# Layer 0 of a four-layer network: products with B and C taken for two tiles at once, through one PSUM tile of two halves

## The chip, the cores and the metric

The kernel runs on one core of a Trainium2 chip. The metric is the device time of one execution in microseconds (us). The core has five engines that work side by side, each through its own instructions in order: TensorE (PE, matrix products into PSUM), VectorE (DVE), ScalarE (ACT), GpSimd (POOL) and SyncE (SP), whose queue here issues the DMA transfers. PSUM is the small memory that TensorE writes; VectorE and ScalarE read and write it too. SBUF is the large on-chip memory. An engine that needs another's result waits on a semaphore for it, and everything behind it in its own queue waits too.

## What is computed

The input is x of shape (4, 96, 64, 64). Four layers follow each other. The change touches only the first, a block of two Mamba layers over sequences of L = 4096 positions, with 192 channels and 16 states per channel. Cut to what matters:

```
for i in range(2):
    h  = layernorm(seq) * ln_g + ln_b
    xs, z = split(h @ in_w)
    xc = silu(causal_conv4(xs) + conv_b)
    dt, Bm, Cm = split(xc @ xproj_w)            # 6, 16, 16 columns
    delta = softplus(dt @ dt_w + dt_b)
    dA  = exp(delta[..., None] * A)             # 192 channels x 16 states
    dBx = delta[..., None] * Bm[:, :, None, :] * xc[..., None]
    hstates = scan(h_t = dA_t * h_{t-1} + dBx_t)
    y   = einsum(hstates, Cm) + Dp * xc
    seq = seq + (y * silu(z)) @ out_w
out = batchnorm(fus_w @ concat(seq, gp(x)) + fus_b) + x
```

The three layers after it (a convolution with an MLP, an attention with a quantized MLP, a Fourier mixer with a quantized MLP) are the same in both kernels.

## The kernel before, in words

Everything is in 32-bit floating point in layer 0. The sequence is cut into pieces of T = 1024 positions. The work is a list of 32 items, one for each batch entry b (4), piece s (4) and Mamba layer i (2). Within an item the 192 channels x 16 states are 24 tiles of 128 partitions by 1024 columns: p (0 to 2) picks 64 channels, j (0, 1) one half of these, g (0 to 3) four of the states, so that a tile holds 32 channels x 4 states. The eight tiles of a p are taken in the order of the list `eight`, here (g, j) = (0,0), (0,1), (3,0), (1,1), (1,0), (3,1), (2,0), (2,1).

For each tile, `exp` (L464) makes dA on ACT from a replicated delta (ddb). The product delta * xc * B is made in one of two ways. On 16 tiles of an item, `rep` (L450) spreads four rows of B over the partitions with two matrix products of 512 columns each (four matmul records) into PSUM, and `scan` (L482) multiplies with the replicated delta * xc (udb) on VectorE, into PSUM. On the eight tiles in `pool_tiles` (2, 5, 7, 10, 13, 15, 18, 21), GpSimd makes the product in SBUF (`times_b`, L470, from udb and brep), and dA goes to PSUM instead (dap). Then `scan` runs the recurrence on VectorE (L486) into hs. `times_c` (L492) multiplies hs with C on GpSimd, in place, `sum_y` (L511) adds over states on PE, `gate` (L522) multiplies with silu(z) on VectorE, and `project` (L529, L224) and `finish` bring the item back to the sequence.

In PSUM there are two tiles of 1024 columns with one buffer each: tag "x" for rep, tag "u" for dap and for those products that are not written over rep. A group of tiles that share B starts at the tiles in `group_starts` (0, 3, 6, 8, 11, 14, 16, 19, 22): there `rep` is filled anew, nine times in an item.

`first_stage` prepares an item ahead: layer norm (L276 to L321), convolution (`parts_of` "xc"), xproj, delta, z, the transfers of delta and delta * xc to memory (dd, ud) and back, spread over the partitions (`load_d`), and of B and C (`load_b`, `load_c`). Its steps have slots; slot t of an item stands 24 steps before step t of that item. Weights and constants are set up before that by `prepare`.

The order on PE, VectorE, ACT and GpSimd is the program's own, written out by hand: the last loop of `layer0` goes over m, one step for each tile, and at each step calls scan(m), rep or exp for tile m+1, exp for tile m+3, times_c for tile m-1, the state copy (`keep_state`) for m-3, times_b by `b_slots`, then sum_y, gate, project and finish of the item at hand, and the steps of `first_stage` that are due. SP's order follows from the order of the calls. Waits are put in by the framework from what each instruction reads and writes in which tile.

Of the kernel before, what the change touches and what calls it, by code (L numbers as in the profile page):

```python
# [50 lines left out]
class Net:  # L51
# [43 lines left out]
    def layer0(self, dram, scratch):  # L95
        tc, nc, ins = self.tc, self.nc, self.ins
        x_in = ins["x"]
        with ExitStack() as ctx:
            cp = ctx.enter_context(tc.tile_pool(name="l0c", bufs=1))
            psum = ctx.enter_context(tc.tile_pool(name="l0p", bufs=2, space=PSUM))  # L100
            psum_x = ctx.enter_context(tc.tile_pool(name="l0x", bufs=1, space=PSUM))
            psum_y = ctx.enter_context(tc.tile_pool(name="l0y", bufs=2, space=PSUM))
# [11 lines left out]
            def wide(rows, cols, k):  # L114
                return psum_x.tile([128, T], F32, name="w_ps", tag="xu"[k % 2])[:rows, :cols]
# [113 lines left out]
            def global_pool():  # L229

                for b in range(B):
                    for s in range(NSC):
                        xt = wk.tile([128, T + 1], F32, name="gp_x", tag="hs", bufs=9)[:C, :T]
                        nc.sync.dma_start(xt, x_in[b, :, s * T : (s + 1) * T])
                        k = b * NSC + s
                        nc.vector.reduce_sum(pooled[:, k : k + 1], xt, axis=mybir.AxisListType.X)
                    yield
                pool4 = cp.tile([C, B], F32, name="pool4")
                nc.vector.reduce_sum(pool4, pooled.rearrange("p (b s) -> p b s", b=B), axis=mybir.AxisListType.X)
                ps = small(C, B)  # L240
                nc.tensor.matmul(ps, gpw, pool4, start=True, stop=True)
                gp = cp.tile([C, B], F32, name="gp")
                nc.scalar.activation(gp, ps, AF.Relu, scale=1.0 / L, bias=self.v("gp_b"))
                yield
                ps = small(C, B)
                nc.tensor.matmul(ps, fus[:, 1, :], gp, start=True, stop=True)
                nc.scalar.activation(fbias, ps, AF.Identity, bias=self.v("fus_b"))
                yield
# [6 lines left out]
            def first_stage(k):  # L255
# [11 lines left out]
                @at_slot(-11)  # L267
                def _():
                    m["xn"] = load_x(b, s, i) if k else x0


                @at_slot(-6)
                def _():
                    m["ps"] = [tile_ps(128), tile_ps(128)]
                    for q in range(8):
                        nc.tensor.matmul(  # L276
                            m["ps"][q // 4][:, q % 4 * C : q % 4 * C + C],
                            m["xn"][:, q * 128 : q * 128 + 128],
                            self.center,
                            start=True,  # L280
                            stop=True,
                        )

                @at_slot(-5)
                def _():
                    m["nt"] = cp.tile([128, 8, C], F32, name="nt", tag="nt")
# [11 lines left out]
                @at_slot(-4)  # L298
                def _():
                    for q in range(8):  # L300
                        x = m["ps"][q // 4][:, q % 4 * C : q % 4 * C + C]
                        nc.scalar.mul(m["nt"][:, q], x, m["rs"][:, q : q + 1])

                @at_slot(-3)
# [7 lines left out]
                @at_slot(-2)  # L312
# [23 lines left out]
                parts_of("xc", [(w_x[:, i, k], k) for k in range(4)], n, ((-1, 1), (0, 2), (2, 4)), 2)  # L336

                @at_slot(4)
                def _():
                    nc.scalar.activation(m["xc"], m["xc"], AF.Silu)  # L340
                    exp_set()

# [3 lines left out]
                @at_slot(7)  # L346
# [4 lines left out]
                @at_slot(8)  # L351
# [6 lines left out]
                parts_of("delta", [(dtw[:, i], 0)], dbl, ((9, 10), (9, 10), (10, 11)), 1)  # L358

                @at_slot(11)  # L360
# [4 lines left out]
                parts_of("z", [(w_z[:, i], 3)], n, ((11, 12), (12, 13), (13, 14)), 3)  # L365

                @at_slot(12)
                def _():
                    m["dd"] = dram.tile([DIN, T], F32, name="dd", tag="dd", bufs=2)
                    for at, rows in both:  # L370
                        nc.sync.dma_start(m["dd"].rearrange("(p c) t -> c p t", p=3)[:, :, at], m["delta"][rows])

                def du(p):
                    if p == 0:
                        m["ud"] = dram.tile([DIN, T], F32, name="ud", tag="ud", bufs=2)
                    of = slice(p, p + 1)
                    u = wk.tile([128, 1, MB], F32, name="du", tag="du")
                    nc.gpsimd.tensor_mul(u, m["delta"][:, of], m["xc"][:, of])  # L378
                    to = m["ud"].rearrange("(p c) t -> c p t", p=3)[:, of]
                    for at, rows in both:  # L380
                        nc.sync.dma_start(to[:, :, at], u[rows])

                for p in range(3):
                    at_slot(14 + 3 * p)(lambda p=p: du(p))

                @at_slot(16)
                def _():
                    nc.scalar.activation(m["z"], m["z"], AF.Silu)
                    exp_set()


                for p in range(3):
                    for j in range(2):
                        at_slot((16, 24, 32)[p] + j)(lambda p=p, j=j: load_d(m, "dd", p, j))
                        at_slot((18, 26, 34)[p] + j)(lambda p=p, j=j: load_d(m, "ud", p, j))
                for g, t in ((0, 10), (1, 21), (3, 23), (2, 25)):
                    at_slot(t)(lambda g=g: load_c(m, g))
                at_slot(19)(lambda: load_b(m, 3))
                at_slot(15)(lambda: load_b(m, 2))
                return steps  # L400

# [9 lines left out]
            def load_c(made, g):  # L411
                made["crep", g] = load_s(made, "crep", NST + 4 * g, 5)
# [4 lines left out]
            def load_d(made, k, p, j):  # L417

                t = wk.tile([128, T], F32, name=f"{k}b", tag=f"{k}b", bufs=4)
                row = 64 * p + 32 * j  # L420
                for s4 in range(4):
                    nc.sync.dma_start(t[32 * s4 : 32 * s4 + 32], made[k][row : row + 32])
                made[k, p, j] = t
# [5 lines left out]
            eight = [(0, 0), (0, 1), (3, 0), (1, 1), (1, 0), (3, 1), (2, 0), (2, 1)]  # L429
            order = [(p, g, j) for p in range(3) for g, j in eight]  # L430
            pool_tiles = (2, 5, 7, 10, 13, 15, 18, 21)
            group_starts = (0, 3, 6, 8, 11, 14, 16, 19, 22)
            NTL = len(order)
# [9 lines left out]
            def rep(m):  # L443

                k, t = divmod(m, NTL)
                x = psum_x.tile([128, T], F32, name="rep", tag="x")
# [6 lines left out]
                return x  # L453

            def exp(m):
# [3 lines left out]
                if on_pool(m):  # L459
                    da = psum_x.tile([128, T], F32, name="dap", tag="u")  # L460
# [5 lines left out]
            def times_b(m):  # L466
                k, t = divmod(m, NTL)
                h, g, j = order[t]
                u = made[k]["u", t] = wk.tile([128, T], F32, name="up", tag="up", bufs=2)
                nc.gpsimd.tensor_mul(u, made[k]["ud", h, j], made[k]["brep", g])  # L470

            def scan(m, x):
# [4 lines left out]
                if on_pool(m):  # L477
                    u = made[k].pop(("u", t))
                else:

                    u = x if on_pool(m + 1) else psum_x.tile([128, T], F32, name="u", tag="u")
                    nc.vector.tensor_mul(u, made[k]["ud", h, j], x)  # L482
                hs = made[k]["hs", t] = wk.tile([128, T + 1], F32, name="hs", tag="hs", bufs=9)
# [4 lines left out]
            def times_c(m):  # L488

                k, t = divmod(m, NTL)  # L490
                hs = made[k]["hs", t]
                nc.gpsimd.tensor_mul(hs[:, :T], hs[:, 1:], made[k]["crep", order[t][1]])  # L492

            def keep_state(m):
                k, t = divmod(m, NTL)
                b, s, i = items[k]
                col = column(t)
                if s < NSC - 1:
                    nc.scalar.copy(state[:, b, i, col : col + 1], made[k]["hs", t][:, T:])
# [5 lines left out]
            def sum_y(k, t0):  # L505

                for q, at in enumerate(halves):
                    for t in (t0, t0 + 1):
                        p, g, j = order[t]
# [4 lines left out]
                            made[k]["hs", t][:, at],  # L514
# [40 lines left out]
            b_slots = {2: 5, 4: 7, 7: 10, 9: 13, 12: 15, 15: 18, 18: 21, 23: NTL + 2}  # L555
# [3 lines left out]
            for m in sorted(stages[0])[:4]:  # L559
                for f in stages[0].pop(m):  # L560
                    f()
            prepare()
            wk = ctx.enter_context(tc.tile_pool(name="l0w", bufs=1))
            with tc.manual_schedule(engines=engines):
                gp = global_pool()
                first = min(stages[0])
                for m in range(first, last + 19):
                    k, t = divmod(m, NTL)
                    if 0 <= m < last:
                        scan(m, x)  # L570
                    if 0 <= m + 1 < last:
                        if on_pool(m + 1):
                            exp(m + 1)
                        elif (t + 1) % NTL in group_starts:
                            x = rep(m + 1)
                    if 0 <= m + AHEAD < last and not on_pool(m + AHEAD):
                        exp(m + AHEAD)
                    if 1 <= m <= last:
                        times_c(m - 1)
                    if 3 <= m < last + 3:  # L580
                        keep_state(m - 3)
                    if -1 <= m and t in b_slots and m - t + b_slots[t] < last:
                        times_b(m - t + b_slots[t])
                    for k0 in range(max(k - 1, 0), min(k + 1, len(items))):
                        at = m - NTL * k0
                        for p in range(3):
# [3 lines left out]
                            if at - 8 * p in (4, 6, 8, 10):  # L590
                                sum_y(k0, at - 4)
                            if at == 8 * p + 11:
                                gate(k0, p)
                        if at == 34:
                            made[k0]["x"] = load_x(*items[k0])
                        if at == 39:
                            project(k0)
                        if at == 41:
# [4 lines left out]
                    if m in (-20, -17, -14, -11, 15, 16):  # L603
# [878 lines left out]
```

## Time and profile before

| | us |
|---|---|
| median of three runs | 3914.21 (3908.41 to 3924.87) |
| profiled execution | 3925.66 |
| its span, first to last instruction | 3923.9 |
| PE busy in the span | 3205.9 (82%) |
| VectorE busy | 3154.4 (80%) |
| ACT busy | 2420.6 (62%) |
| GpSimd busy | 2911.4 (74%) |
| first scan of layer 0 starts | 77.3 |
| last scan of layer 0 ends | 2612.5 |

The page of the profile gives the busy time of each engine over the whole span, so it mixes layer 0 with the three others. Layer 0 takes the first two thirds. What the change does to it is read from stretches inside layer 0 and from groups of instructions that occur only there. A group's line reads: line of the kernel, engine, operation, the tile written <- the tiles read, shapes, count | busy us, mean ns of one | idle time of the engine just before them, and who ended it. "<-DVE hs L486 428.3" behind a group thus means that its engine stood idle for 428.3 us in total until a scan at L486 let it go. Idle time of an engine costs something only if another one then waits for it.

### The profile page before, as it was taken

The numbers are of one execution on the slowest core, as the hardware profiler recorded it, in microseconds if no ns is written. First come the engines' busy times: TensorE is split into PE (matmuls) and PEld (weight loads), VectorE is DVE, ScalarE is ACT, GpSimd is POOL, SyncE is SP. The second block draws the span as 40 slices with busy tenths as digits, with TensorE's granted clock in tenths as the row PEclk, the third lists the DMA queues.
The fourth block names the chain that finished last, engine by engine and source line by source line (L and its number), as shares of the span: only waits on it lengthen the run. The fifth ranks groups of instructions, "written<-read, shape, count | busy, mean of one in ns | idle before, by whom it ended". The sixth has DMA issues, their size and how long they took to land. (4 is left out here: it accounts for less than half of the span.)

```text
span 3923.9 us, 43975 instructions
## 1 busy us (share of the span) xinstructions
PE 3205.9 (82%) x13534; PEld 1294.8 (33%) x13534; DVE 3154.4 (80%) x2772; ACT 2420.6 (62%) x4644; POOL 2911.4 (74%) x1443
## 2 busy tenths in 40 slices
PE   6887878877878788877878887755899988899988
PEld 3222222222222222222222222115644534666643
DVE  5999999999999999999999999973374385444649
ACT  4666667766766676666766666532254676666557
POOL 2999999999999999999999999961101064444427
PEclk7788878898788888888878878766899999999989
DMA  7567656675666566756676566636300000011101
GB/s 188 135 162 171 151 130 168 164 170 131 164 158 173 132 165 154 172 140 158 153 171 150 143 161 163 159 90 211 140 1 0 1 1 6 15 36 33 39 7 59
DMA packets 179828, 463.31 MB, mean 118 GB/s; under 512 B 52852, under 2 KB 54782, under 8 KB 176256
## 3 DMA queue, kind: packets, MB, share of 16 engines
q1 hardware_dynamic: 179592, 460.49, 46.7%
q8 instruction: 108, 1.77, 0.2%
q14 instruction: 128, 1.05, 0.1%
HBM read 386.81 MB, written 73.50 MB: 117 GB/s over the span
## 5 line engine op out<-in xcount | busy, mean ns | idle before, releaser
L492 POOL TENSOR_TENSOR hs<-hs,crep 128x1024 f32<-128x1024 f32 x768 | 1797.7, 2364 | 48.0 <-DVE hs L486 26.1
L450 PE MATMUL rep<-dbl,sel_b 32*128 32x512 f32 x1152 | 407.8, 785 | 495.8 <-DVE hs L486 428.3
L464 ACT ACTIVATE da<-ddb,nega 128x1024 f32<-128x1024 f32 x512 | 584.9, 1150 | 47.2 <-DVE hs L486 40.0
L470 POOL TENSOR_TENSOR up<-udb,brep 128x1024 f32<-128x1024 f32 x256 | 605.2, 2364 | 8.8 <-DMA brep<-cd 8.8
L464 ACT ACTIVATE dap<-ddb,nega 128x1024 f32<-128x1024 f32 x256 | 286.0, 1117 | 409.3 <-DVE hs L486 408.5
L511 PE MATMUL y<-hs,sel_r 128*32 128x512 f32 x3072 | 476.4, 690 | 5.5 <-POOL hs L492 5.5
L486 DVE TENSOR_TENSOR_SCAN hs<-da,state,rep 128x1024 f32<-128x1024 f32 x192 | 450.8, 2348 | 16.7
L486 DVE TENSOR_TENSOR_SCAN hs<-da,state,u 128x1024 f32<-128x1024 f32 x192 | 450.9, 2348 | 11.2 <-DVE u L482 1.4
L486 DVE TENSOR_TENSOR_SCAN hs<-dap,state,up 128x1024 f32<-128x1024 f32 x192 | 446.7, 2326 | 0.4 <-ACT dap L464 0.4
L210 PE MATMUL ps<-n,w_x 97*64 97x512 f32 x1536 | 408.0, 679 | 9.3 <-ACT n L319 6.6
L482 DVE TENSOR_TENSOR u<-udb,rep 128x1024 f32<-128x1024 f32 x256 | 314.7, 1229 | 74.4 <-PE rep L450 46.0
L450 PEld LDWEIGHTS rep<-dbl,sel_b 32*128 32x128 f32 x1152 | 107.0, 214 | 794.5 <-issue 595.7
L482 DVE TENSOR_TENSOR rep<-udb,rep 128x1024 f32<-128x1024 f32 x256 | 310.3, 1212 | 0.2
L1040 POOL CAST hq<-y 128x1536 fp8e5<-128x1536 f16 x64 | 94.0, 1469 | 219.3 <-issue 122.6
L210 PEld LDWEIGHTS ps<-n,w_x 97*64 97x64 f32 x1536 | 118.6, 153 | 295.2 <-issue 243.5
L511 PEld LDWEIGHTS y<-hs,sel_r 128*32 128x32 f32 x3072 | 65.2, 114 | 336.5 <-issue 208.5
L378 POOL TENSOR_TENSOR du<-delta,xc 128x512 f32<-128x512 f32 x96 | 122.6, 1277 | 64.7 <-ACT delta L362 50.2
L914 POOL MEMSET h<- 1x4096 f32 x1 | 3.5, 3507 | 212.8 <-DVE n L820 212.8
L1179 POOL TENSOR_TENSOR av<-av,ec 128x780 f32<-128x780 f32 x32 | 58.8, 1837 | 133.2 <-ACT av L1176 133.2
L486 DVE TENSOR_TENSOR_SCAN hs<-da,rep 128x1024 f32<-128x1024 f32 x64 | 146.5, 2289 | 5.4
L224 PE MATMUL ps<-xc,xproj 64*102 64x512 f32 x384 | 147.3, 924 | 3.5 <-ACT xc L340 3.5
L486 DVE TENSOR_TENSOR_SCAN hs<-da,u 128x1024 f32<-128x1024 f32 x64 | 146.4, 2288 | 3.7 <-DVE u L482 0.5
(262 smaller groups left out, 6137.7 us busy)
## 6 DMA issues: line engine op xcount, KB each, us to landing
ddb<-dd SPq DMA_DIRECT2D x768, 128.0 KB
udb<-ud SPq DMA_DIRECT2D x768, 128.0 KB
crep<-cd SPq DMA_DIRECT2D x512, 128.0 KB
brep<-cd SPq DMA_DIRECT2D x256, 128.0 KB
dd<-delta SPq DMA_DIRECT2D x64, 384.0 KB
ud<-du SPq DMA_DIRECT2D x192, 128.0 KB
band<-in_band SPq DMA_DIRECT2D x24, 1024.0 KB
x<-in_x SPq DMA_DIRECT2D x32, 384.0 KB
```

Of the source, the lines that this page charges most:

```text
L210: nc.tensor.matmul(ps[rows], w[:, 64 * p : 64 * p + 64], rhs[:, at.start + shift : at.stop + shift], start=k == 0, stop=k == len(ws) - 1, ...
L224: nc.tensor.matmul(ps, w[rows, p], x[rows, p], start=start and p == 0, stop=p == 2)
L378: nc.gpsimd.tensor_mul(u, m["delta"][:, of], m["xc"][:, of])
L450: nc.tensor.matmul(x[:, at], sel_b[rows, order[t][1]], made[k]["dbl"][rows, at], start=True, stop=True)
L464: nc.scalar.activation(da, made[k]["dd", h, j], AF.Exp, scale=nega[:, col : col + 1])
L470: nc.gpsimd.tensor_mul(u, made[k]["ud", h, j], made[k]["brep", g])
L482: nc.vector.tensor_mul(u, made[k]["ud", h, j], x)
L486: nc.vector.tensor_tensor_scan(hs[:, 1:], made[k].pop(("da", t)), u, 0.0 if s == 0 else st, ALU.mult, ALU.add)
L492: nc.gpsimd.tensor_mul(hs[:, :T], hs[:, 1:], made[k]["crep", order[t][1]])
L511: nc.tensor.matmul(made[k]["y", p][row : row + 32], sel_r, made[k]["hs", t][:, at], start=False, stop=True, skip_group_check=True,)
L1040: nc.gpsimd.tensor_copy(q, y2, saturate=False)
L1179: nc.gpsimd.tensor_add(v[:, 2:4], v[:, 0:2], ec)
```

## The change

All of it is in layer 0. Tiles j = 0 and j = 1 of the same p and g share B and C. The change takes their products together:

- On GpSimd, `times_c` becomes one instruction for both tiles of a (p, g): 12 of 2 x 1024 columns in an item in place of 24 of 1024. hs becomes a tile of two halves, five buffers in place of nine single ones. `times_b` takes both tiles of g = 3 in one instruction, and the one GpSimd tile of g = 2 for p = 0 and 1 alone. du is one product of 1536 columns, written over delta, in place of three of 512.
- On VectorE, the product with rep is one of 2048 columns for the six pairs in `paired`; single ones stay for tiles 6, 14, 22 and 23. The order in `eight` has (1,0) before (1,1).
- In PSUM, the tiles "x" and "u" become one tile `pair` of two halves of 1024 columns: rep is written into half 1, dap into half 0, a paired product over both.
- `first_stage` starts two slots earlier, its later steps are shifted among each other, silu(z) of an item is joined to the silu of the next item's xc (four ACT table loads an item in place of six), `load_u` brings both j of delta * xc at once (two pair buffers in place of four single ones), each C row group has a buffer of its own (four in place of five shared), z has two buffers in place of three, and nt shares a buffer with the single product of `times_b`.
- `sum_y` and `gate` come some steps later, `project` and `finish` four steps earlier; the state is copied for two tiles at once.

```diff
+            pair_ps = psum_x.tile([128, 2, T], F32, name="pair")
...
-                        xt = wk.tile([128, T + 1], F32, name="gp_x", tag="hs", bufs=9)[:C, :T]
+                        xt = wk.tile([128, 2, T + 1], F32, name="gp_x", tag="hs", bufs=5)[:C, 0, :T]
...
-                    m["nt"] = cp.tile([128, 8, C], F32, name="nt", tag="nt")
+                    if k:
+                        nt = wk.tile([128, T], F32, name="nt", tag="up2")
+                    else:
+                        nt = first_pool.tile([128, T], F32, name="nt")
+                    m["nt"] = nt[:, : 8 * C].rearrange("p (q c) -> p q c", q=8)
...
-                parts_of("xc", [(w_x[:, i, k], k) for k in range(4)], n, ((-1, 1), (0, 2), (2, 4)), 2)
-
-                @at_slot(4)
+                parts_of("xc", [(w_x[:, i, k], k) for k in range(4)], n, ((-3, -1), (-2, 0), (0, 2)), 2)
+
+                @at_slot(2)
                 def _():
                     nc.scalar.activation(m["xc"], m["xc"], AF.Silu)
+                    if k:
+                        silu_z(k - 1)
                     exp_set()
...
-                for p in range(3):
-                    at_slot(14 + 3 * p)(lambda p=p: du(p))
-
-                @at_slot(16)
-                def _():
-                    nc.scalar.activation(m["z"], m["z"], AF.Silu)
-                    exp_set()
+                    nc.gpsimd.tensor_mul(m["delta"], m["delta"], m["xc"])
+                    spread_out("delta", "ud")
+
+                parts_of("z", [(w_z[:, i], 3)], n, ((14, 15), (14, 15), (15, 16)), 2)
 
                 for p in range(3):
                     for j in range(2):
-                        at_slot((16, 24, 32)[p] + j)(lambda p=p, j=j: load_d(m, "dd", p, j))
-                        at_slot((18, 26, 34)[p] + j)(lambda p=p, j=j: load_d(m, "ud", p, j))
-                for g, t in ((0, 10), (1, 21), (3, 23), (2, 25)):
+                        at_slot((15, 22, 31)[p] + j)(lambda p=p, j=j: load_d(m, p, j))
+                    at_slot((16, 24, 31)[p])(lambda p=p: load_u(m, p))
+                for g, t in ((0, 21), (1, 24), (3, 25), (2, 27)):
                     at_slot(t)(lambda g=g: load_c(m, g))
...
+            def load_u(made, p):
+                t = made["ud", p] = wk.tile([128, 2, T], F32, name="udb", tag="udb", bufs=2)
+                for j in range(2):
+                    fetch_rows(t[:, j], made["ud"], p, j)
...
-            eight = [(0, 0), (0, 1), (3, 0), (1, 1), (1, 0), (3, 1), (2, 0), (2, 1)]
+            eight = [(0, 0), (0, 1), (3, 0), (1, 0), (1, 1), (3, 1), (2, 0), (2, 1)]
...
+            paired = (0, 3, 8, 11, 16, 19)
+            ends = {1: 0, 4: 1, 5: 3, 7: 2}
...
             def rep(m):
...
-                x = psum_x.tile([128, T], F32, name="rep", tag="x")
+                x = pair_ps[:, 1]
...
                 if on_pool(m):
-                    da = psum_x.tile([128, T], F32, name="dap", tag="u")
+                    da = pair_ps[:, 0]
...
+            def times_b(k, p, g):
+
+                u = made[k]["ud", p]
+                if g == 3:
+                    up = wk.tile([128, 2, T], F32, name="up3", tag="up3", bufs=2)
+                    made[k]["up", p, 3, 0], made[k]["up", p, 3, 1] = up[:, 0], up[:, 1]
+                    nc.gpsimd.tensor_mul(up, u, twice(made[k]["brep", 3]))
+                else:
+                    up = made[k]["up", p, g, 1] = wk.tile([128, T], F32, name="up2", tag="up2")
+                    nc.gpsimd.tensor_mul(up, u[:, 1], made[k]["brep", g])
+
+            def scan(m):
...
-                    u = x if on_pool(m + 1) else psum_x.tile([128, T], F32, name="u", tag="u")
-                    nc.vector.tensor_mul(u, made[k]["ud", h, j], x)
-                hs = made[k]["hs", t] = wk.tile([128, T + 1], F32, name="hs", tag="hs", bufs=9)
+                    u = pair_ps[:, 1 if on_pool(m + 1) else 0]
+                    nc.vector.tensor_mul(u, made[k]["ud", h][:, j], pair_ps[:, 1])
...
+                elif t in paired:
+                    u = pair_ps[:, 0]
+                    nc.vector.tensor_mul(pair_ps, made[k]["ud", h], twice(pair_ps[:, 1]))
+                elif t - 1 in paired:
+                    u = pair_ps[:, 1]
...
-            def times_c(m):
-
-                k, t = divmod(m, NTL)
-                hs = made[k]["hs", t]
-                nc.gpsimd.tensor_mul(hs[:, :T], hs[:, 1:], made[k]["crep", order[t][1]])
+            def times_c(k, p, g):
+
+                hs = made[k]["hs", p, g]
+                nc.gpsimd.tensor_mul(hs[:, :, :T], hs[:, :, 1:], twice(made[k]["crep", g]))
...
-            b_slots = {2: 5, 4: 7, 7: 10, 9: 13, 12: 15, 15: 18, 18: 21, 23: NTL + 2}
+            b_slots = {3: (0, 1, 3), 4: (0, 0, 2), 11: (0, 2, 3), 12: (0, 1, 2), 20: (1, 0, 3)}
...
-                            if at - 8 * p in (4, 6, 8, 10):
-                                sum_y(k0, at - 4)
-                            if at == 8 * p + 11:
+                            if at - 8 * p in (5, 8, 10, 12):
+                                sum_y(k0, p, {5: 0, 8: 1, 10: 3, 12: 2}[at - 8 * p])
+                            if at == 8 * p + 15:
                                 gate(k0, p)
...
-                        if at == 39:
+                        if at == 35:
                             project(k0)
-                        if at == 41:
+                        if at == 37:
                             finish(k0)
```

## The prediction

> **What bounds the kernel now.** I read, in order, the busy times by stretch, the groups by line and shape, the waits, and the order of time around one reload of rep. First the stretches inside layer 0 (columns: length, busy time of PE, PEld, DVE, ACT and POOL, clock, DMA share, GB/s):
>
> ```profile
> 1000.00:1500.00 500.00, 403.52 (x1650) 116.76 (x1646) 477.96 (x271) 336.76 (x672) 489.76 (x222) 0.81 0.63 158
> ```
>
> GpSimd is busy 489.8 of 500 us and VectorE 478.0: GpSimd sets the pace, with VectorE 12 us behind. The groups say with what:
>
> ```profile
> L492 POOL TENSOR_TENSOR hs<-hs,crep 128x1024 f32<-128x1024 f32 x768 | 1797.7, 2364 | 48.0 <-DVE hs L486 26.1 <-issue 15.3 <-POOL hs L492 2.7
> L470 POOL TENSOR_TENSOR up<-udb,brep 128x1024 f32<-128x1024 f32 x256 | 605.2, 2364 | 8.8 <-DMA brep<-cd 8.8
> L486 DVE TENSOR_TENSOR_SCAN hs<-dap,state,up 128x1024 f32<-128x1024 f32 x192 | 446.7, 2326 | 0.4 <-ACT dap L464 0.4
> L450 PE MATMUL rep<-dbl,sel_b 32*128 32x512 f32 x1152 | 407.8, 785 | 495.8 <-DVE hs L486 428.3 <-DVE u L482 67.6
> L482 DVE TENSOR_TENSOR u<-udb,rep 128x1024 f32<-128x1024 f32 x256 | 314.7, 1229 | 74.4 <-PE rep L450 46.0 <-DMA udb<-ud 9.6
> L464 ACT ACTIVATE dap<-ddb,nega 128x1024 f32<-128x1024 f32 x256 | 286.0, 1117 | 409.3 <-DVE hs L486 408.5
> ```
>
> Tile t of an item takes a product (L482; not on the eight "GpSimd" tiles) and a scan (L486) on VectorE. PE waits 428 us for scans before it refills rep, and ACT 408 us before it writes dap; but VectorE waits back only 46 us and 0.4 us. Both refills are early. The order of time shows why (columns: start, length, engine and line):
>
> ```profile
> 1001.36 1.21 DVE L482 TENSOR_TENSOR rep<-udb,rep 128x1024 f32<-128x1024 f32 x1
> 1001.48 1.12 ACT L464 ACTIVATE dap<-ddb,nega 128x1024 f32<-128x1024 f32 x1 [1.38 <-DVE hs L486]
> ...
> 1002.67 2.35 DVE L486 TENSOR_TENSOR_SCAN hs<-da,state,rep 128x1024 f32<-128x1024 f32 x1
> ...
> 1004.93 2.33 DVE L486 TENSOR_TENSOR_SCAN hs<-dap,state,up 128x1024 f32<-128x1024 f32 x1
> ...
> 1005.16 1.13 PE L450 MATMUL rep<-dbl,sel_b 32*128 32x512 f32 x4 [1.12 <-DVE hs L486]
> ...
> 1007.36 1.23 DVE L482 TENSOR_TENSOR u<-udb,rep 128x1024 f32<-128x1024 f32 x1
> ```
>
> dap (tile "u") is written while VectorE works on rep (tile "x"), and rep is refilled inside the dap scan. Two PSUM tiles let the refills pass each other. The same refill can cost twice as much:
>
> ```profile
> 1015.29 2.08 PE L450 MATMUL rep<-dbl,sel_b 32*128 32x512 f32 x4 [4.16 <-DVE hs L486]
> ```
>
> That is 2.08 us after 4.16 us of idle PE, against 1.13.
>
> **Period now.** The first scan starts at 77.3 and the last ends at 2612.5: 32 items of 79.2 us. GpSimd's two products at 1001.74 last to 1006.40, 2.33 each from start to start, and a 512-column du takes 1.24: 32 x 2.33 + 3 x 1.24 = 78.3 us an item. VectorE's starts add to 77.6.
>
> [...] the rows say 1212 and 1229. [...] I take 2.31 us. [...] the trace's slope, (2.33-1.24)/512, is 2.13 ns. [...]
>
> **The change, part by part.** *GpSimd.* Its fixed part is 2.33 - 1024 x 0.00213 = 0.15 us. After: 15 products of 2048 columns at 4.51, two of 1024, one du of 1536 at 3.42: 67.7 + 4.7 + 3.4 = 75.7 us an item, 2.6 less (83 us in 32). *VectorE.* Twelve products become six of 2.31; with 0.05 to the next start, 6 x 2.36 + 4 x 1.30 + 24 scans x 2.26 + 3 gates x 0.58 = 75.3 us. *ACT.* Six table loads become four (2 x 1.28 us less) and the state copies are halved: ACT is busy 336.8 of 500 us, so this hides behind VectorE.
>
> *The wait that is added.* rep and dap become the halves of one PSUM tile, pair. In the program as built, waits are taken against the whole tile. The matmul (L461) that fills half 1 for tile 3 waits for the VectorE count of the scan of tile 2, which reads only half 0; before, it waited for the scan of tile 1. The exponential that fills half 0 for tile 2 waits for the scan of tile 1, which reads only half 1, and for rep's matmul. So it stands for all nine refills of rep and all eight of dap in an item: scan, exponential, scan, matmul, product now follow each other. Queued behind the waiting scan on VectorE are all later products and scans; behind the waiting matmul on PE sum_y and the stage's matmuls; behind the waiting exponential on ACT the exponentials of later tiles and the stage's copies. GpSimd waits for the scans and sum_y for GpSimd, both with slack once the steps are longer; the one who has none is VectorE itself.
>
> From the trace: scan end to exponential 0.035 us, to rep 0.145; exponential end to scan 0.10, rep end to product 0.045. With R for a refill of rep:
> - two paired tiles and a GpSimd tile: product to scan 2.36, scan 2.26, second scan to dap's scan 2.35+0.035+1.12+0.10 = 3.60, dap's scan to product 2.33+0.145+R+0.045 = 2.52+R. Sum 10.74+R, six times.
> - single tile and GpSimd tile: 1.30+3.60+2.52+R = 7.42+R, twice.
> - tiles 22 and 23: 1.30+2.41+1.28+2.54+R = 7.53+R.
>
> That is 86.8 + 9R; gates lie under the refills. R: PE has some 49 us of other work an item and waits most of the rest. Beside project (tiles 11-14), the convolution parts (22-0) and xproj (3-6) it is warm, 1.13; at the other six it has idled about 4 us or more, and all thirteen refills in the trace after some 4 us or more took 2.08, those after 1 to 3.5 us either length. 9R = 6 x 2.08 + 3 x 1.13 = 15.9. PE is in order and itself late twice: after the refill for 22 stand one sum_y and two convolution parts (1.0-1.9 + 2 x 3.65) against 7.5 us of chain, after that for 11 project (3.73+4.10) and three small steps against 10.7. I take 2 + 1 us. Period: 86.8 + 15.9 + 3.0 = 105.7.
>
> *Buffers and moved steps,* costed at nothing. GpSimd has 30 us of slack an item, which covers pair latency (an hs pair waits for both scans; five pairs hold ten tiles, nine before), the single crep buffers and the du that now waits for dd to land. udb is loaded in pairs: eight issues take 3.6 us on SP, and p=1 goes out at step 0, once tile 23's product has freed the older pair, for GpSimd at step 3, some 11 us later. If that cover were gone, GpSimd, then sum_y on PE, would be late by the landing. SP waits at ud for du, with brep and ddb behind it, needed eight steps later. z (three buffers to two) is rewritten at slot 15, after project at step 11; nt shares up2 and follows tile 15's scan; the two joined Silus hold ACT 5.5 us between exponentials some 11 us apart. PE's order moves too (convolution parts at steps 21, 22 and 0, project at 11): that is in the lateness above. The start may move by 10 us either way: there the gp_x loads share the queues with the first item's, through five buffers in place of nine.
>
> **Sum.** 32 x 105.7 = 3382, less 11 because the first eight items carry no state (scans 0.06 shorter): 3371 against 2535, +836 us. Profiled execution 3925.7 (span 3923.9): 4762. The median of the three runs (3914.2) is 11 us below the profiled one: I say 4750, 21% slower.
>
> **Rivals.**
> *PE stays warm and is never late:* period 86.8 + 9 x 1.13 = 97.0, +558 us, about 4475. For it: many refills after 1 to 3 us of idle took 1.13. Against: the thirteen after 4 us or more.
> *PE cold throughout, later still:* 86.8 + 18.7 + 5 = 110.5, +990, about 4905. For it: steps get further apart, so idle grows. Against: project and the convolution parts are 7 us of continuous work.
> *Other side, the halves run apart:* if a refill starts 0.15 us after the last scan of its own half, nothing is exposed, GpSimd's 75.7 plus today's 0.9 us give 76.6: 2.6 x 32 = -83 us, 3831. For it: the GpSimd sum[...]. Against: the built waits. It decides where less than 79.2 - 75.3 = 3.9 us an item is exposed; I count 30.
> *GpSimd bounds:* it would have to take (105.7-3.4-4.7)/15 = 6.5 us for a product, 3.2 ns a column against 2.13; a repeated operand has no row in the trace, so I bound it between 4.4 (no fixed cost) and that. Nothing speaks for it.
>
> **How the numbers follow.** Forecast 0.70 (own range 4620 to 4890), warm PE 0.15, cold and late 0.09, GpSimd 0.02, apart 0.04. A range of 4560 to 4910 keeps the forecast, most of the cold case and the upper part of the warm one: about 8 in 10. Slower by over 0.5% 0.96, within 0.5% 0.01, faster 0.03; 0.5% is about what a measurement of this kernel tells from no change.
>
> **What would show it.** Right: VectorE waits about 1.3 us for ACT before nearly all 256 dap scans (some 330 us) and 1.3 to 2.3 us for PE before the 288 products that follow a refill; GpSimd's share in the stage falls to about 72%; refills of 2.08 us are the majority; 2048-column products near 2.31 and 4.51 us. Wrong: a refill that starts during the scan before it, or GpSimd still near 98%.

## The result and the profile after

The changed kernel takes 4811.06 us (median of 4 runs, 4805.26 to 4813.54) against 3916.86 us before (3908.41 to 3924.87): a ratio of 1.228, with a 95% interval of 1.225 to 1.231. The forecast was 4750 us, with a range of 4560 to 4910.

Inside layer 0 the two engines that were busy almost all the time are so no more. The busy times of one stretch (length, then PE, PEld, DVE, ACT and POOL, clock, DMA share, GB/s):

```profile
1000.00:1500.00 500.00, 343.92 (x1252) 92.52 (x1252) 357.20 (x174) 232.09 (x419) 333.55 (x84) 0.73 0.47 116
```

GpSimd fell from 489.8 to 333.6 us of 500 and VectorE from 478.0 to 357.2. What they do costs no more than before; they wait. The groups by line and shape:

```profile
L515 POOL TENSOR_TENSOR hs<-hs,crep 128x2048 f32<-128x2048 f32 x384 | 1597.2, 4170 | 1121.5 <-DVE hs L510 886.3
L461 PE MATMUL pair<-dbl,sel_b 32*128 32x512 f32 x1152 | 513.5, 983 | 1086.5 <-DVE hs L510 1081.1
L474 ACT ACTIVATE pair<-ddb,nega 128x1024 f32<-128x1024 f32 x256 | 286.2, 1118 | 1265.0 <-DVE hs L510 1265.0
L499 DVE TENSOR_TENSOR pair<-udb,pair 128x2048 f32<-128x2048 f32 x192 | 440.9, 2296 | 444.4 <-PE pair L461 442.2
L485 POOL TENSOR_TENSOR up<-udb,brep 128x2048 f32<-128x2048 f32 x96 | 435.0, 4531 | 24.6 <-DMA crep<-cd 23.8
```

Before, VectorE's products waited 46.0 us for rep; now the double ones alone wait 442.2 us (25.2 of them once, before the first product of all). The waits (engine, line, released by: us in total, times, longest) add the single products and the dap scans:

```profile
DVE hs L510 <- ACT pair L474: 321.6, 255, 1.7
DVE pair L504 <- PE pair L461: 186.6, 95, 2.8
```

In the kernel before, the 256 dap scans waited 1.8 us in all for the exponential. The order of time around one dap tile shows the chain itself (start, length, engine, line, idle before and its releaser):

```profile
2012.21 4.59 DVE L510 TENSOR_TENSOR_SCAN hs<-da,state,pair 128x1024 f32<-128x1024 f32 x2
2016.89 1.12 ACT L474 ACTIVATE pair<-ddb,nega 128x1024 f32<-128x1024 f32 x1 [7.58 <-DVE hs L510]
...
2018.12 2.35 DVE L510 TENSOR_TENSOR_SCAN hs<-pair,state,up 128x1024 f32<-128x1024 f32 x1 [1.32 <-ACT pair L474]
2020.52 2.07 PE L461 MATMUL pair<-dbl,sel_b 32*128 32x512 f32 x4 [6.20 <-DVE hs L510]
2022.64 2.29 DVE L499 TENSOR_TENSOR pair<-udb,pair 128x2048 f32<-128x2048 f32 x1 [2.18 <-PE pair L461]
```

Scan, exponential, scan, matmul, product: each begins when the one ahead of it ends. In the kernel before, the exponential ran under the product ahead and the refill inside the dap scan.

**Where the time is.** The first scan of layer 0 starts at 109.9 us (before 77.3), the last ends at 3494.3 (before 2612.5). The 32 items take 3384.4 us, 105.8 each, against 2535.2 us, 79.2 each: +849.2 us. The start is 32.6 us later, and what follows layer 0 is 2.2 us shorter. These three sum to the spans' difference, 4803.5 - 3923.9 = 879.6 us.

The 32.6 us are no part of the chain in the items. PE and GpSimd before the first product:

```profile
91.72 4.50 POOL L485 TENSOR_TENSOR up<-udb,brep 128x2048 f32<-128x2048 f32 x1 [23.76 <-DMA crep<-cd]
96.15 0.10 POOL L320 MEMSET n<- 97x3 f32 x1
```

```profile
96.31 10.10 PE L211 MATMUL ps<-n,w_x 97*64 97x512 f32 x32 [25.71 <-POOL n L320]
106.33 1.13 PE L461 MATMUL pair<-dbl,sel_b 32*128 32x512 f32 x4
```

GpSimd waits for the pair udb, whose transfers are issued from 83.9 us on (the line names one of crep, which this product does not read). It takes its double product, and only then clears the first three columns of n for the next item. PE's convolution for that item waits 25.7 us for that memset, and the first refill of rep stands behind the convolution on PE.

Some 6 us come earlier, and from the one tile again. `prepare` made its weights in the two PSUM tiles in turn; now it makes them in the two halves of pair in turn. The activation that completes the first delta ends at 58.8 us against 52.8 before. With one tile in the kernel before (experiment 1) it ends at 59.2, with two tiles in the changed kernel (experiment 2) at 51.8.

### The profile page after: what moved, and what is told of

It is laid out like the page before. It is cut to its first block, busy times and chain, and to the rows that moved or that the text cites. A ratio compares the mean times of both kernels' runs of the same rounds, so it can differ in the third digit from the quotient of the medians.

```text
span 4803.5 us, 42016 instructions
## 1 busy us (share of the span) xinstructions
PE 3485.5 (73%) x13534; PEld 1316.9 (27%) x13534; DVE 3148.8 (66%) x2580; ACT 2324.7 (48%) x4294; POOL 2704.8 (56%) x899
## 5 line engine op out<-in xcount | busy, mean ns | idle before, releaser
L515 POOL TENSOR_TENSOR hs<-hs,crep 128x2048 f32<-128x2048 f32 x384 | 1597.2, 4170 | 1121.5 <-DVE hs L510 886.3
L461 PE MATMUL pair<-dbl,sel_b 32*128 32x512 f32 x1152 | 513.5, 983 | 1086.5 <-DVE hs L510 1081.1
L510 DVE TENSOR_TENSOR_SCAN hs<-da,state,pair 128x1024 f32<-128x1024 f32 x384 | 885.6, 2338 | 23.1 <-DVE pair L504 0.5
L474 ACT ACTIVATE pair<-ddb,nega 128x1024 f32<-128x1024 f32 x256 | 286.2, 1118 | 1265.0 <-DVE hs L510 1265.0
L499 DVE TENSOR_TENSOR pair<-udb,pair 128x2048 f32<-128x2048 f32 x192 | 440.9, 2296 | 444.4 <-PE pair L461 442.2
L510 DVE TENSOR_TENSOR_SCAN hs<-pair,state,up 128x1024 f32<-128x1024 f32 x192 | 451.3, 2350 | 242.2 <-ACT pair L474 240.9
L474 ACT ACTIVATE da<-ddb,nega 128x1024 f32<-128x1024 f32 x512 | 581.0, 1143 | 20.6 <-DMA ddb<-dd 14.9
L485 POOL TENSOR_TENSOR up<-udb,brep 128x2048 f32<-128x2048 f32 x96 | 435.0, 4531 | 24.6 <-DMA crep<-cd 23.8
L211 PE MATMUL ps<-n,w_x 97*64 97x512 f32 x1536 | 399.5, 675 | 26.9 <-POOL n L320 25.7
L510 DVE TENSOR_TENSOR_SCAN hs<-da,pair 128x1024 f32<-128x1024 f32 x128 | 287.6, 2278 | 7.2
L525 PE MATMUL y<-xc,dp 128*128 128x512 f32 x192 | 166.4, 963 | 0.0
L488 POOL TENSOR_TENSOR up<-udb,brep 128x1024 f32<-128x1024 f32 x64 | 150.4, 2350 | 0.0
```

The costliest lines, as they stand in the source:

```text
L211: nc.tensor.matmul(ps[rows], w[:, 64 * p : 64 * p + 64], rhs[:, at.start + shift : at.stop + shift], start=k == 0, stop=k == len(ws) - 1, ...
L461: nc.tensor.matmul(x[:, at], sel_b[rows, order[t][1]], made[k]["dbl"][rows, at], start=True, stop=True)
L474: nc.scalar.activation(da, made[k]["dd", h, j], AF.Exp, scale=nega[:, col : col + 1])
L485: nc.gpsimd.tensor_mul(up, u, twice(made[k]["brep", 3]))
L488: nc.gpsimd.tensor_mul(up, u[:, 1], made[k]["brep", g])
L499: nc.vector.tensor_mul(pair_ps, made[k]["ud", h], twice(pair_ps[:, 1]))
```

## The experiments

**1. The kernel before, with its two PSUM tiles made halves of one.** The weights of `prepare` are made in the halves as well. Nothing else is changed: no double product, no other buffer, no moved step.

```
+            pair_ps = psum_x.tile([128, 2, T], F32, name="pair")
...
-                return psum_x.tile([128, T], F32, name="w_ps", tag="xu"[k % 2])[:rows, :cols]
+                return pair_ps[:rows, k % 2, :cols]
...
-                x = psum_x.tile([128, T], F32, name="rep", tag="x")
+                x = pair_ps[:, 1]
...
-                    da = psum_x.tile([128, T], F32, name="dap", tag="u")
+                    da = pair_ps[:, 0]
...
-                    u = x if on_pool(m + 1) else psum_x.tile([128, T], F32, name="u", tag="u")
+                    u = x if on_pool(m + 1) else pair_ps[:, 0]
```

> The kernel before, with only its two PSUM tiles made halves of one; no paired product, nothing moved. Theory: the same chain appears with single products: 88.2 + 9 x 1.79 + 3 = 107.3 us an item in place of 79.2, +899 less 11 for the items without state: about 4800 us (4650 to 4950), first scan still at 77 us. Rival (the paired products, buffers or moved steps cause the loss): 3917 us, as before.

Measured: 4810.27 us, ratio 1.229 (1.225 to 1.233); 106.9 us an item, first scan at 83.7 us where 77 was expected. Its waits:

```profile
DVE pair L483 <- PE pair L451: 495.7, 258, 2.2
DVE hs L487 <- ACT pair L465: 289.9, 217, 2.0
```

The one tile alone makes a loss of the same size; the double products, buffers and moved steps are not needed for it. The expected sum is met, but not term by term. PE is never late here (each refill starts 0.1 us or less after the scan ahead, on the mean), where 3 us an item had been put in; instead the three gates do not lie under a refill (1.7 us an item), and the exponential holds a dap scan up by 1.36 us in place of 1.26 (0.9 us an item).

**2. The changed kernel with two PSUM tiles.** With two tiles no double product is left, and VectorE takes 16 single ones. The weights of `prepare` have two tiles again, too.

```
-                x = pair_ps[:, 1]
+                x = psum_x.tile([128, T], F32, name="rep", tag="x")
...
-                    da = pair_ps[:, 0]
+                    da = psum_x.tile([128, T], F32, name="dap", tag="u")
...
-                elif t in paired:
-                    u = pair_ps[:, 0]
-                    nc.vector.tensor_mul(pair_ps, made[k]["ud", h], twice(pair_ps[:, 1]))
...
+                    u = x if on_pool(m + 1) else psum_x.tile([128, T], F32, name="u", tag="u")
+                    nc.vector.tensor_mul(u, made[k]["ud", h][:, j], x)
```

> The changed kernel with two PSUM tiles, as before, and so with 16 single products on VectorE in place of six double and four single ones; GpSimd's double products, the buffers and the moved steps stay. Theory: VectorE's 77.6 us an item sets the pace with little lost, 78 us: 32 x 78 = 2496 against 2535, plus 32 us of later start: about 3910 us (3860 to 3990). Rival (double products on GpSimd, udb pairs, hs pairs or moved steps cost what was measured): well above 4000.

Measured: 3942.96 us, ratio 1.008 (1.005 to 1.011); 78.8 us an item, first scan at 101.3 us. The loss in the items is gone. What is left of the change gains 0.4 us an item and loses 24 us at the start, 8.6 us less than with one tile.

**3. The changed kernel with its halves apart.** The tile and the double products stay. Each access to pair by a refill, an exponential, a product or a scan is listed with the half it touches; the waits between accesses to different halves are dropped, and those within a half are stated anew.

```
+                    if not (h0 & halves_of):
+                        tc.declare_no_dep(ins.ins, old, reason="other half of pair, other banks")
+                    elif write or w0:
+                        tc.add_manual_dep(
+                            ins.ins, old.name, mybir.DependencyInfo(mybir.DependencyClass.Sync, mybir.DependencyReason.DATA), reason="same half"
+                        )
...
-                    nc.vector.tensor_mul(pair_ps, made[k]["ud", h], twice(pair_ps[:, 1]))
+                    touch(nc.vector.tensor_mul(pair_ps, made[k]["ud", h], twice(pair_ps[:, 1])), {0, 1}, True)
```

> The changed kernel, with the waits between the two halves of pair dropped and all waits within a half kept. Theory (the loss is the waits taken against the whole PSUM tile): nothing of the chain scan, exponential, scan, matmul, product is exposed any more; VectorE's own 75.3 us an item plus a little, say 76, sets the pace, so 32 x (105.8 - 76) = 950 us go: about 3860 us (3810 to 3930), the start still 32 us late. VectorE's waits for ACT and for PE fall from 322 and 629 us to under 60 in all. Rival (the chip itself keeps the halves in order, or wide products, paired loads and moved steps cost the time): 4500 us or more.

Measured: 3910.98 us, ratio 0.9994 (0.998 to 1.001): all of the loss is gone, and 50 us of the expected gain are missing. After the first product VectorE waits 52 us in all for the refills and no longer for the exponentials. The order of time inside layer 0:

```profile
2004.23 2.33 DVE L528 TENSOR_TENSOR_SCAN hs<-pair,state,up 128x1024 f32<-128x1024 f32 x1
...
2004.38 2.08 PE L476 MATMUL pair<-dbl,sel_b 32*128 32x512 f32 x4 [3.90 <-DVE hs L528]
...
2007.06 2.29 DVE L516 TENSOR_TENSOR pair<-udb,pair 128x2048 f32<-128x2048 f32 x1
2009.38 4.59 DVE L528 TENSOR_TENSOR_SCAN hs<-da,state,pair 128x1024 f32<-128x1024 f32 x2
2011.76 1.12 ACT L489 ACTIVATE pair<-ddb,nega 128x1024 f32<-128x1024 f32 x1 [1.07 <-DVE hs L528]
```

PE refills half 1, even in 2.08 us, while the scan reads half 0, and ACT writes half 0 while the second scan reads half 1. The chip runs the two side by side: the refill from 2004.38 to 2006.46 lies inside the scan from 2004.23 to 2006.56, which takes 2.33 us (2.35 on the mean in the changed kernel), and the exponential beside the second scan takes 1.12 us, as there. The waits alone had kept them in order. That the halves lie in different banks, as the edit's reason says, is not shown. From the ninth on the items take mostly 76.7 us, where 76 were expected. But items 2 to 6 take 82. PE before a refill in the second item, VectorE's product behind that refill, and GpSimd:

```profile
175.42 9.85 PE L211 MATMUL ps<-n,w_x 97*64 97x512 f32 x32 [0.75 <-POOL n L320]
185.19 1.13 PE L476 MATMUL pair<-dbl,sel_b 32*128 32x512 f32 x4
```

```profile
186.37 2.29 DVE L516 TENSOR_TENSOR pair<-udb,pair 128x2048 f32<-128x2048 f32 x1 [3.91 <-PE pair L476]
```

```profile
170.80 4.52 POOL L502 TENSOR_TENSOR up<-udb,brep 128x2048 f32<-128x2048 f32 x1 [1.20 <-DMA udb<-ud]
175.28 0.09 POOL L320 MEMSET n<- 97x3 f32 x1
```

It is the same memset as at the start. It is made for the eight items of the sequences' first pieces.

**4. The memset of n on VectorE,** alone, and together with the halves apart.

```
-                        nc.gpsimd.memset(n[:, :3], 0.0)
+                        nc.vector.memset(n[:, :3], 0.0)
```

> The changed kernel with only the memset of n on VectorE in place of GpSimd. Theory: the first product starts at 92 us, when udb has landed, in place of 107.5; the items stay bound by the chain at 105.8 us: 4811 - 15 = about 4796 us (4785 to 4803). Rival (the late start has another cause): first product still at 107 us, 4811.

Measured alone: 4797.36 us, ratio 1.225 (1.222 to 1.229). The first product starts at 92.4 us in place of 107.5, and the items stay at the chain's pace: the memset carries 15 of the 32.6 us.

> The changed kernel with the waits between the halves of pair dropped and the memset of n (first piece of each sequence, the first eight items) on VectorE in place of GpSimd. Theory: with the halves apart the memset stands behind GpSimd's double product, PE's convolution and the refill of rep behind it wait for it; without that the first product waits for udb alone (91.7 us in place of 107.8, -15) and items 2 to 6 fall from 82 to 77 us (-25 to -30): 3911 - 45 = about 3866 us (3845 to 3890), below the kernel before. Rival (the 82 us of these items and the late start have another cause): 3911 us as without it.

Measured together: 3873.07 us, ratio 0.989 (0.987 to 0.991), faster than both kernels. First scan at 96.4 us, 77.0 us an item; the first eight items take 28.7 us less than without the moved memset. The remaining 19 us of the start stay. Some 6 are the weights of `prepare` in the one tile. For the rest: in the changed kernel the first udb pair is issued at 83.9 us against 70.0 before, on SP behind the transfer of du, which GpSimd starts only when the transfer of delta has landed (64.5 us). That this explains the rest is argued; no run tried to shorten it.

**5. One half of the waits at a time.** The same edit as in 3, with the waits dropped only of the refills of rep, or only of the exponentials into dap.

```
                     if not (h0 & halves_of):
+                        if ins.ins.engine != mybir.EngineType.PE:
+                            continue
                         tc.declare_no_dep(ins.ins, old, reason="other half of pair, other banks")
```

(For dap, `Activation` stands in place of `PE`.)

> The changed kernel with only the waits of rep's refills on the other half dropped; the exponentials into dap still wait across. Theory: nine refills of 1.79 us and nine wake-ups of 0.19 go off the chain, and PE's lateness of up to 3 us: 18 to 21 us an item, 570 to 665 us: about 4200 us (4130 to 4260). Rival (one exposed refill only covers the other, and the chain re-forms through dap): 4500 us or more.

Measured: 4247.47 us, ratio 1.085 (1.082 to 1.088), 88.3 us an item: 17.5 off, just under the 18 to 21 expected. VectorE's waits for PE are down to 35.7 us and those for dap stay:

```profile
DVE hs L530 <- ACT pair L491: 296.6, 236, 1.7
DVE pair L518 <- PE pair L478: 21.2, 25, 3.6
DVE pair L524 <- PE pair L478: 14.5, 20, 1.3
```

> The changed kernel with only the waits of the dap exponentials on the other half dropped; rep's refills still wait across. Theory: eight times 1.26 us (0.035 + 1.12 + 0.10) go off the chain, 10.1 us an item, 323 us: about 4490 us (4440 to 4540). Rival (the shorter steps leave PE late or change what the refills cost): PE warmer and refills shorter, down to 4380; or the exponential is hidden only in part, above 4600.

Measured: 4377.16 us, ratio 1.118 (1.114 to 1.122), 92.3 us an item: 13.5 off where 10.1 were expected, and the time is below the expected range; the rival of a warmer PE ("down to 4380") meets it. The waits for ACT are gone and those for PE are shorter:

```profile
DVE pair L518 <- PE pair L478: 375.6, 191, 4.4
DVE pair L524 <- PE pair L478: 150.6, 95, 3.9
```

They sum to 526 us. The 629 us of the changed kernel have the 25.2 us before the first product among them, which this trace puts down to a transfer; without these the waits are 77 us shorter, 2.4 us an item. The refills' mean goes down from 1.78 to 1.62 us (busy time of the matmul group over 288), which is 1.5 us of that. PE being less late is the other 1 us: counted over the traces, the refills for tiles 0 and 14 start 2.4 and 0.6 us after the scan ahead in place of 2.9 and 1.1. The exponentials themselves give 10.7 us, not 10.1: a dap scan started 1.26 us after the end of the scan ahead, and now starts 0.08 us before it, as scans do that need not wait. That is 13.1 of the 13.5. 17.5 + 13.5 is 31.0, and both together take off 27.8 (105.8 to 77.9): the 2.4 us at the refills are in both, and the rest of the difference is about what the memset costs the early items.

**6. dap in SBUF.** Another way to free pair: the exponential goes into the ring of da.

```
-                    da = pair_ps[:, 0]
+                    da = wk.tile([128, T], F32, name="dap", tag="da", bufs=AHEAD + 1)
```

> The changed kernel with dap in an SBUF buffer (the ring of da) in place of half 0 of pair, so that nobody writes pair between the products but rep. Theory: the refill of rep waits for the scan before the dap scan and hides under the dap scan, the exponential waits for nothing: VectorE bound at 76 us an item, about 3860 us (3810 to 3960), if a scan with both inputs in SBUF costs the 2.3 us it costs with one in PSUM. Rival: such a scan and GpSimd's products slow each other; each 0.3 us on the 8 scans of an item adds 77 us to the whole.

Measured: 4321.73 us, ratio 1.105 (1.101 to 1.108), 90.6 us an item. The rival holds: the scan is 1.5 us dearer, where each 0.3 us had been priced at 77 us of the whole:

```profile
L515 POOL TENSOR_TENSOR hs<-hs,crep 128x2048 f32<-128x2048 f32 x384 | 1965.2, 5145 | 147.0 <-DMA crep<-cd 108.3
L510 DVE TENSOR_TENSOR_SCAN hs<-dap,state,up 128x1024 f32<-128x1024 f32 x192 | 728.7, 3795 | 0.5 <-ACT dap L474 0.5
```

A dap scan takes 3.80 us in place of 2.33, and GpSimd's product 5.15 in place of 4.17. Single ones show how:

```profile
2000.35 6.39 DVE L510 TENSOR_TENSOR_SCAN hs<-dap,state,up 128x1024 f32<-128x1024 f32 x1
...
2023.13 2.33 DVE L510 TENSOR_TENSOR_SCAN hs<-dap,state,up 128x1024 f32<-128x1024 f32 x1
```

```profile
2000.05 4.54 POOL L485 TENSOR_TENSOR up<-udb,brep 128x2048 f32<-128x2048 f32 x1
...
2023.43 6.04 POOL L515 TENSOR_TENSOR hs<-hs,crep 128x2048 f32<-128x2048 f32 x1 [4.48 <-DMA crep<-cd]
```

The scan at 2000.35 starts within a GpSimd product that ends at 2004.59, and ends at 2006.74, 2.15 us after it. The scan at 2023.13 finds GpSimd idle and takes 2.33; the GpSimd product that starts inside it takes 1.9 us longer than the usual 4.17. In both cases the one that starts second gets on as if it began only at the end of the first, to some 0.2 us: the scan ends 2.15 us after the product's end, against 2.33 alone, and the product 4.01 us after the scan's end, against 4.17. With dap in PSUM neither holds the other up: in the changed kernel the dap scan at 2018.12 takes 2.35 us inside a GpSimd product that starts at 2017.02 and takes its 4.17. What in the chip keeps the two apart is not shown.

**7. The same, with GpSimd nearly idle.** The product with C covers 32 of every 1024 columns; the rest of that product is left out.

```
...
-                nc.gpsimd.tensor_mul(hs[:, :, :T], hs[:, :, 1:], twice(made[k]["crep", g]))
+                nc.gpsimd.tensor_mul(hs[:, :, :32], hs[:, :, 1:33], twice(made[k]["crep", g][:, :32], 32))
```

> The kernel with dap in SBUF, and GpSimd's product with C cut to the first 32 of every 1024 columns (the rest of hs stays without C: most of that product is left out), so that GpSimd is idle for most of an item. Theory (a scan with both inputs in SBUF and a GpSimd product slow each other while both run): the dap scans that meet no GpSimd product take 2.3 us, their mean falls from 3.8 to under 2.8 (three 4.5 us products an item are left), and VectorE alone bounds: about 3850 us (3800 to 3930). Rival (such a scan costs 3.8 us by itself): 3.8 us stays, and the time stays above 4100 us.

Measured: 3938.75 us (one run), first scan at 110.7 us. The dap scans are back at 2.50 us on the mean, so the form costs next to nothing where no product is met:

```profile
L510 DVE TENSOR_TENSOR_SCAN hs<-dap,state,up 128x1024 f32<-128x1024 f32 x192 | 480.2, 2501 | 0.1
```

A small GpSimd product against such a scan shows this at its plainest (VectorE, then GpSimd):

```profile
1507.80 2.33 DVE L510 TENSOR_TENSOR_SCAN hs<-dap,state,up 128x1024 f32<-128x1024 f32 x1
```

```profile
1500.63 0.31 POOL L515 TENSOR_TENSOR hs<-hs,crep 128x64 f32<-128x64 f32 x1 [2.29 <-DVE hs L510]
1508.06 2.18 POOL L515 TENSOR_TENSOR hs<-hs,crep 128x64 f32<-128x64 f32 x1 [7.12 <-DVE hs L510]
```

Free, it takes 0.31 us; started inside the scan, it ends 0.11 us after it. The time is 89 us over the expectation and just above its range. The first six items take 82 us, as in 3. Of the later ones, eleven take 80 to 82 us where the others take some 76.5, and in each of these the dap scan of tile 21 meets a double product with B, which is still done in full, and takes 2.9 to 6.4 us. VectorE also waits once in each of them 1.2 to 3.5 us for a refill; the cause of that was not sought.

**8. The output of the double product with B in rows of 1025.**

```
-                    up = wk.tile([128, 2, T], F32, name="up3", tag="up3", bufs=2)
+                    up = wk.tile([128, 2, T + 1], F32, name="up3", tag="up3", bufs=2)[:, :, :T]
```

> The changed kernel with the output of the double product with B in rows of 1025 in place of one run of 2048, as hs has them. If the form of the output sets GpSimd's time, this product falls from 4.53 us to the 4.17 us that the product with C takes; if what is read or that hs is worked in place sets it, 4.53 us stays. The time stays at 4811 us in both cases, since GpSimd waits for the scans.

Measured: 4811.96 us (one run), and the product stays as it was:

```profile
L485 POOL TENSOR_TENSOR up<-udb,brep 128x2048 f32<-128x2048 f32 x96 | 435.2, 4533 | 24.5 <-DMA crep<-cd 23.4
```

The form of the output is not what makes the product with C faster. What does, its input in rows of 1025 or that it works in place, stays open.

## Why the prediction was right, and where its sum was off

**The wait against the whole tile** was the right cause. One tile in the old kernel brings the loss (4810 us), and dropping those waits in the new one takes it away (3911 us).

**The chain, 86.8 + 9R + 3.0 = 105.7 us an item,** measured 105.8 on the mean of all items and 106.2 in the 24 that carry a state, for which the sum was made. dap's scans waited 1.26 us each for ACT, 255 of 256 times, 321.6 us in all against "some 330". The products waited 629 us for PE over 286 times, 25.2 of them at the start; the others are 2.1 us on the mean. Counted over the trace, the time from the end of a scan through the refill to the product is 20.8 us an item, where the forecast had 20.6: 9R = 15.9, 3.0 for PE's lateness, and nine times 0.19 for the wake-ups.

Within these 20.6 us several terms are off and cancel. R was taken as 15.9 / 9 = 1.77 us and is 1.78; of 288 refills 176 took about 2.1 us, so the cold ones (some 2.1 us against 1.13 warm) are the majority. In this trace none of the 200 that follow 3 us or more of idle PE took 1.13 us; 63 of the 68 that follow less than 2 us did. Those for tiles 0 and 14 are warm, as said (1.13 us in 31 of 32 each). But that for tile 6, taken as warm, has a mean of 1.62, and that for tile 22, taken as cold, one of 1.77. PE is late at the two places that were named, for tile 0 (2.9 us after the scan) and tile 14 (1.1 us), by more than the 2 and 1 us taken; the other seven refills start 0.05 us after their scan, not 0.145. The mechanism is the one forecast; that its sum fits to 0.2 us is in part luck. The double product is 2.296 us. The 2.31 of the forecast was an estimate; two rows of the kernel before, 666 ns at 512 columns (L522) and 1212 at 1024 (L482), carried on in a straight line give 2.30.

**GpSimd** was mis-sized with no effect on the sum: its double product with C takes 4.17 us and not 4.51, while the one with B takes 4.53. So an item costs it 12 x 4.17 + 3 x 4.53 + 2 x 2.35 + 3.43 = 71.8 us and not 75.7, and its share in the stage is 67%, not 72%. The rival that needs 6.5 us is excluded by these rows.

**The start** is the term that failed: "10 us either way", measured +32.6 us. The step looked only at transfers that share the queues. It left out an instruction queued behind another on GpSimd: the memset of n behind the first double product, which waits for a pair where a single tile had sufficed, and on PE the convolution and the first refill behind that. The memset run gave back 15 us of it. And it left out that `prepare` makes its weights in the same tile: some 6 us. What makes the rest is argued above, not shown.

**The number.** The forecast was 61 us low: 13 from the loop (849 against 836), 33 from the start, -2 after layer 0, and some 17 from the step from the profiled execution to the median (-12 taken from the kernel before; for the kernel after the median is 6 us above its profiled execution).

**The rivals.** Warm PE (97.0 us an item) falls by the mean refill of 1.78 us, cold PE throughout (110.5) by the 105.8. The other side, halves apart, priced at 3831 us, is not what the kernel does; but made to be so, it gave 3911, and 3873 with the memset moved. Its price missed the start and the slow early items. Its pace, 76.6 us an item, is met by the quiet items (76.7), but by luck: it was reckoned from GpSimd, which then needs only 71.8, and VectorE sets it.

**The covers costed at nothing** held in the loop: with the halves apart the quiet items take 76.7 us, 1.4 above VectorE's own 75.3, so the udb pairs, the hs pairs, the single buffers and the table loads cost next to nothing there. The memset of n, which costs the early items time, was not among those named.

## What to carry to other kernels

Before two buffers are joined for the sake of one wider instruction, look at how the waits are built: where they are taken against the whole tile, joining ends every overlap between the halves, and that cost 26.6 us an item here for a saving of some 2.3 on VectorE and 6.5 on GpSimd. If the wide instruction is wanted, state which half each access touches. And follow small instructions too: a 0.1 us memset that is queued behind an instruction made longer, with another engine waiting for it, cost 15 us at the start here, and another 29 us in the first eight items once the halves were apart.

## What was not expected of the hardware

- GpSimd's product of 2 x 1024 columns takes 4.17 us in place, and 4.53 us from udb and brep into another buffer; two single ones took 2 x 2.36. That the output's rows are not the cause is shown; the cause is open.
- The scan with both inputs in SBUF and GpSimd's products exclude each other in these traces: 6.39 us for a scan of 2.33, and 2.18 us for a product of 0.31. With dap in PSUM the scan takes 2.33 us on the mean beside GpSimd in the kernel before, and 2.35 in the changed one, against 3.80 with dap in SBUF. The place of dap in PSUM is what keeps the two engines out of each other's way here; the cause is open.
